# Layer 1 in the order of every fourth token, layer 0 entries turned by DMA, and new latencies in the list of a four-layer graph kernel

## The chip, the cores and the metric

One core of one Trainium2 chip. The time is the device time of one execution in microseconds; for the kernel before it is the median of three runs, 1753.9 us (1751.21 to 1754.06).

## The reference

Input x holds 32 graphs of 512 tokens with 128 features; adj is one 512 x 512 matrix of zeros and ones for all of them. Each of four layers computes x = x + layer(relu(layernorm(x)), adj).

```python
# layer 0: attention by edges
x_h = elu(x @ Wi + bi)
a_src, a_tgt = x_h @ We[:H, 0], x_h @ We[H:, 0]
e = sigmoid(a_tgt[:, :, None] + a_src[:, None, :] + be) * (adj + ALPHA * (adj == 0))
recv = elu(concat([einsum('bij,bjh->bih', e, x_h), x_h * e.sum(-1, keepdims=True)]) @ Wn + bn)
out = concat([recv, x_h]) @ Wm + bm
# layer 1: a gated unit, five steps (in_matrix = out_matrix = adj)
m = adj @ h;  av = concat([m, m]);  u3 = h @ u3_w.T + u3_b
z = sigmoid(av @ w3_w.T + w3_b + u3);  r = sigmoid(av @ w4_w.T + w4_b + u3)
hv = tanh(av @ w5_w.T + w5_b + (r * h) @ u5_w.T + u5_b);  h = (1 - z) * h + z * hv
# layer 2: adj @ (x @ weight) + bias
# layer 3: sum over k = 0..3 of adj^k @ x @ V_k, V_k folded from weight_1
```

## The kernel before, in words

All tensors stay in fp32; x of four graphs (a group, G = 4) lies in one "x" buffer of [128, 4, 4, 128], tokens on partitions in four chunks. Inside a layer most tiles are feature-major: features on the 128 partitions, the 512 tokens in the free dimension ("f" buffers, 36 of them; "b" buffers are the eight PSUM banks, "m" and "d" are scratch in DRAM).

**A list, not loops, sets the order.** `Plan.op` (L53) records every operation with its engine, an estimate of its duration, a due time and what it reads and writes. `Plan.order` (L98) then plays the list through: an engine that is free takes the ready operation with the earliest due time for which buffers are free. A result counts as known `RESULT[eng]` (L45) after the operation's end. An operation of DVE that is marked `two` (two inputs in SBUF) and any of POOL exclude each other in it. The instructions are then issued in that order on every engine. The due times come from `begin(b)` (L560), from PACE, FIRST_PACE and LAST_PACE (L217) and from offsets in each layer. [...]

**Prefix and arms.** Up to `BRANCH` (30 us of the list) the order is common (L578). In this prefix adj is transposed into A_r (fp32r), a mask is made, and four DVE operations (L424) count elements that fp32r would not hold exactly; all engines read the count `inexact` and branch (L812). Of the two arms the exact one runs with these inputs: each value for an adjacency product is split in fp32r parts `hi` (ACT, L672) and `lo` (DVE, L675), and two single-pass matmuls add up to the product.

**Layer 0** (`layer0`, L455): layernorm (L377 to L404: statistics on DVE, the power on POOL, scaling on ACT), then h is turned to feature-major by four TensorE transposes into a PSUM bank (`transposed`, L324) and an ACT copy (`copied`, L350), and multiplied with Wi (`product`, L355). elu (L440) takes three activations and two DVE operations. For the edges, four times a tanh (L507) and a DVE operation with the mask (L510); POOL adds the four results (L516, three additions). TensorE forms the messages (L525), and one product with ones (L530, graphs 0 to 3; issued at L357) or two fp32r passes (L539, later graphs) form the sum over neighbours; own (L542), Wn (L357), elu, and Wm (L552) follow.

**Layer 1** (`layer1`, L694): h is feature-major. In each of the five steps the adjacency product (L686, eight passes) and u3T (L357) come first, each copied out of PSUM by ACT (L352); then gate r (w4T, L704, L362, L711), gate z (w3T), w5T and u5T into one bank, a tanh, and three DVE operations (L721, L723, L725). `turned` (L333) brings h back to tokens on partitions: one DVE transpose of 32 x 32 blocks (L337), a DMA to scratch (L340) and a DMA back (L342). L337 reads its source with a step of four elements, which is why the blocks' rows are every fourth token.

**Layers 2 and 3** (L737, L751): one adjacency product and a narrow product; and a Horner scheme over k with L760 and L769.

Graphs enter layer 1 at `begin(b)` plus 2.0 PACE, graphs 0 to 3 and the last five at 1.2 PACE (L802).

Of the kernel before, what the change touches and what calls it, by code (L numbers as in the profile page):

```python
# [11 lines left out]
F32R = mybir.dt.float32r  # L12
I32 = mybir.dt.int32
AF = mybir.ActivationFunctionType
ALU = mybir.AluOpType

P = 128
# [21 lines left out]
class Plan:  # L39
# [2 lines left out]

    RESULT = {"PE": 0.5, "ACT": 0.5, "DVE": 0.5, "POOL": 0.6, "SP": 2.5}  # L45

    def __init__(self, slots, ahead, last):
        self.ahead, self.last, self.ops, self.vals = ahead, last, [], {}
# [40 lines left out]
    def back_to(self, state):  # L89
# [5 lines left out]
            )  # L95
        self.free = {k: [*f] for k, f in free.items()}

    def order(self, end=None):  # L98

        left = [o for o in self.ops if not o.begun]  # L100
# [7 lines left out]
        for i, o in enumerate(left):  # L108
            index[o] = i
            o.waits = sum(not b.begun for b in o.before)  # L110
            o.ready = max([0.0, *(b.known for b in o.before if b.begun)])
# [19 lines left out]
        while events:  # L131
            now = heapq.heappop(events)
            if end is not None and now >= end:
                break
            for e in self.until:
                while coming[e] and coming[e][0][0] <= now:
                    _, i, o = heapq.heappop(coming[e])
                    heapq.heappush(ready[e], (o.due, i, o))
                if self.until[e] > now:
                    continue  # L140
                passed, o = [], None
                while ready[e] and o is None:
                    x = heapq.heappop(ready[e])
                    if begins(x[2], now):
                        o = x[2]
                    else:
                        passed.append(x)
                for x in passed:
                    heapq.heappush(ready[e], x)
                if o is None:  # L150
                    continue
                order.append(o)
                o.begun = True
                while oldest + 1 < len(by_due) and by_due[oldest].begun:
                    oldest += 1
                o.start, self.until[e] = now, now + o.us
                if o.two or e == "POOL":
                    self.shared = self.until[e]
                for v in o.takes:
                    v.slot = self.free[v.kind].pop(0)[1]  # L160
                o.known = self.until[e] + o.result
                heapq.heappush(events, self.until[e])
                heapq.heappush(events, o.known)
                for v in o.vals:
                    v.left -= 1
                    if not v.left and v.kind:
                        self.free[v.kind].append((o.known, v.slot))
                        self.free[v.kind].sort()
                for a in o.after:
                    if a in index:  # L170
                        a.waits -= 1
                        a.ready = max(a.ready, o.known)
                        if not a.waits:
                            heapq.heappush(coming[a.eng], (a.ready, index[a], a))
        assert end is not None or len(order) == len(left), "the plan does not end: too few buffers"
# [5 lines left out]
def tile_four_graph_layers(  # L181
# [27 lines left out]
    nc = tc.nc  # L209
# [4 lines left out]
    K = l3_w.shape[2]  # L214
    assert D == P and G * D == 512 and N == 512 and K == 7

    PACE, FIRST_PACE, LAST_PACE = 56.0, 14.0, 30.0  # L217
    BRANCH = 30.0

    T_MM, T_TR, T_NARROW, T_PASS = 0.86, 0.44, 0.224, 0.23  # L220
    T_VEC, T_COPY, T_ACT = 0.61, 0.5, 0.6

    slots = {"x": 6, "f": 36, "q": 4, "s": 8, "d": 4, "m": 8, "b": 8}
    plan = Plan(slots, ahead=60.0, last=(B - 2) * PACE)
    op = plan.op

# [106 lines left out]
    def turned(src, due):  # L333


        blocks, moved, t = Val("f"), Val("m"), Val("f")
        op("DVE", 1.03, due, lambda: nc.vector.transpose(  # L337
            at(blocks).rearrange("p (q c f) -> p q c f", c=NC, f=32),
            at(src).rearrange("p (c i q) -> p q c i", c=NC, q=4)), [src], [blocks])
        op("SP", 1.0, due, lambda: nc.sync.dma_start(at(moved), at(blocks)),  # L340
           [blocks], [moved], result=4.0)
        op("SP", 1.0, due, lambda: nc.sync.dma_start(  # L342
            at(t).rearrange("p (b e) -> p b e", e=P),
            at(moved).rearrange("(b i) (q e) -> (i q) b e", i=32, e=P)), [moved], [t], result=6.0)
        return t

    def by_chunk(t):
# [4 lines left out]
        op("ACT", us, due, lambda: nc.scalar.copy(at(t), at(src)), [src], [t])  # L352
        return t

    def product(w, src, due, dst=None, start=True, stop=True):  # L355
        dst = dst or Val("b")
        op("PE", T_MM, due, lambda: nc.tensor.matmul(  # L357
            at(dst), at(w), at(src), start=start, stop=stop), [src, w], [dst])
        return dst

    def tanh(dst, src, due, bias, scale=0.5, us=T_ACT):
# [45 lines left out]


    A_r, mask = const("A_r", [P, NC, N], F32R), const("mask", [P, NC, N])
    inexact = const("inexact", [1, 1], I32)  # L410
    n_odd = const("n_odd", [P, NC])
    for jc in range(NC):
        pt, z, odd = Val("b"), Val("f"), Val("f")
        def turn(jc=jc, pt=pt):
            for ic in range(NC):
                nc.tensor.transpose(at(pt)[:, ts(ic, P)], at(A_nat[ic])[:, ts(jc, P)], at(ident))
        op("PE", T_TR, jc, turn, [*A_nat, ident], [pt])
        op("ACT", T_COPY, jc, lambda jc=jc, pt=pt: nc.scalar.copy(at(A_r)[:, jc, :], at(pt)),
           [pt], [A_r])
        op("ACT", T_COPY, jc, lambda z=z, pt=pt: nc.scalar.mul(at(z), at(pt), 1 / ALPHA), [pt], [z])  # L420
        op("DVE", T_VEC, jc, lambda jc=jc, z=z, pt=pt: nc.vector.scalar_tensor_tensor(
            at(mask)[:, jc, :], at(pt), 0.0, at(z), op0=ALU.is_equal, op1=ALU.add),
            [pt, z], [mask])
        op("DVE", 0.7, jc, lambda jc=jc, pt=pt, odd=odd: nc.vector.scalar_tensor_tensor(  # L424
            at(odd), at(A_r)[:, jc, :].bitcast(F32), 1.0, at(pt),
            op0=ALU.mult, op1=ALU.not_equal, accum_out=at(n_odd)[:, jc : jc + 1]),
            [A_r, pt], [odd, n_odd])
    p_odd = Val("b")
    def count():
        for jc in range(NC):  # L430
# [4 lines left out]
    op("PE", 0.3, 8, count, [n_odd, ones], [p_odd])  # L435
    op("DVE", 0.2, 8, lambda: nc.vector.tensor_copy(at(inexact), at(p_odd)[:1, :1]),
       [p_odd], [inexact])


# [14 lines left out]

    def layer0(b, h, due):  # L455
        KEEP = 12
        hT = copied(transposed(h, due), due)
        d = due + 6
        xhT = elu(product(Wi_sb, hT, d), bi_sb, bi_half, d, KEEP)

        d = due + 14
        msg, ends = Val("f"), Val("s")
# [42 lines left out]
        for jc in range(NC):  # L505
# [8 lines left out]
        sums = [Val("f"), Val("f")]  # L514
        def add(dst, a, c):
            op("POOL", 1.4, d, lambda: nc.gpsimd.tensor_tensor(  # L516
                at(dst), at(a), at(c), op=ALU.add), [a, c], [dst])
        add(sums[0], es[0], es[1])
        add(sums[1], es[2], es[3])
        add(sums[0], sums[0], sums[1])  # L520

        d = due + 30
        pn = Val("b")
# [3 lines left out]
                [msg, es[jc]], [pn])  # L527

        if b < G:
            ps = product(ones, sums[0], d)  # L530
        else:
            high, low, ps = Val("q"), Val("q"), Val("b")
            op("ACT", T_COPY, d, lambda: nc.scalar.copy(at(high), at(sums[0])), [sums[0]], [high])
            op("DVE", T_VEC, d, lambda: nc.vector.tensor_tensor(
# [54 lines left out]
    def list_rest(exact, pool):  # L589
# [75 lines left out]
        def parts(src, due, two=False, view=None):  # L665
# [3 lines left out]
                return view(at(src)) if view else at(src)  # L669
            def part(v):  # L670
                return at(v).rearrange("p (c b f) -> p c b f", c=NC, f=32) if view else at(v)
            op("ACT", T_COPY, due, lambda: nc.scalar.copy(part(hi), whole()), [src], [hi])  # L672
            if not exact:
                return [hi]
            op("DVE", T_VEC, due, lambda: nc.vector.tensor_tensor(  # L675
# [1 line left out]
                [src, hi], [lo], two=two)  # L677
            return [lo, hi]

        def times_adj(tok, due):  # L680

            pa = Val("b")
            def emit():
                for jc in range(NC):
                    for n, part in enumerate(tok):
                        nc.tensor.matmul(  # L686
                            at(pa), at(part)[:, ts(jc, P)], at(adjT)[:, jc, :],
                            start=jc == n == 0, stop=jc == NC - 1 and n == PARTS - 1,
                        )
            op("PE", NC * PARTS * T_ADJ, due, emit, [*tok, adjT], [pa])  # L690
            return pa


        def layer1(b, h, due, pace):  # L694
            tok = parts(h, due, two=True)
            h = copied(transposed(h, due), due)
            for t in range(STEPS):
                d = due + t * pace
                u = copied(product(u3T, h, d), d)
                m = copied(times_adj(tok, d), d)  # L700

                def gate(wT, bias, d, m=m, u=u):
                    pg, s = product(wT, m, d), Val("f")
# [148 lines left out]
```

## Time and profile before

| what | value |
|---|---|
| median of three runs | 1753.9 us |
| the profiled execution's own time | 1748.12 us |
| its span | 1746.3 us |
| mean granted TensorE clock | 0.994 |
| L686, adjacency of layers 1 and 2 | 1536 matmul records, 421 ns each |
| L357 with u3T, w3T, w4T, w5T, u5T | 320 records each (160 products), 592 to 599 ns |
| L352, ACT copies out of PSUM | 448, 588 ns |
| L516, POOL additions of layer 0 | 96, 1608 ns |
| L399, scaling of layernorm on ACT | 512, 488 ns |

A record of a matmul starts before the one ahead of it has ended, so its duration is longer than the time that it adds; the starts of neighbours tell the latter. One fp32 matmul of 128 x 512 leaves two records. The page divides the span in 40 slices of 43.7 us, and gives for each engine the busy tenths. Groups are given by line, engine and tiles with count, busy us and mean ns, then the idle time of the engine just before them. The chain that ended last is 76% PE.

### The profile page before, as it was taken

Reading aid. Unit: us, or ns where it says so; the run is one execution under the profiler, and the core shown is the slowest. Engines: PE = TensorE matmul, PEld = TensorE weight load, DVE = VectorE, ACT = ScalarE, POOL = GpSimd, SP = SyncE. Lnnn points to the kernel's source line nnn. Section 1 sums busy time; section 2 is a strip of 40 time slices with the busy share of each in tenths; the row PEclk is TensorE's granted clock in tenths of the full one; section 3 lists DMA queues with packets and bytes.
Section 4 is the critical chain, followed back from the end, with each engine's and each line's share of the span. In section 5 each row is a group of like instructions: output and inputs, shape, how many; then the busy total and the mean of one; then the engine's idle time right before and its main releaser. Section 6 shows DMA issues by size and latency. Waiting matters only on the chain.

```text
span 1746.3 us, 21006 instructions
## 1 busy us (share of the span) xinstructions
PE 1695.5 (97%) x6829; PEld 1098.0 (63%) x6829; DVE 1479.3 (85%) x3213; ACT 1135.2 (65%) x2155; POOL 399.8 (23%) x312
## 2 busy tenths in 40 slices
PE   5899999999999999999999999999999999999998
PEld 3555555566666666665666666666666656656797
DVE  6899999999898887888888898888899879878752
ACT  6767765778666666665765667666768656655451
POOL 4521210332222211222212221122232212001110
PEclk9999999999999999999999999999999999999999
DMA  4022322322222222223221221222322131221201
GB/s 109 7 53 75 85 73 73 81 52 85 52 58 61 79 67 46 74 75 55 67 55 60 79 61 61 67 52 81 67 67 55 50 84 61 73 72 58 76 13 48
DMA packets 164534, 112.07 MB, mean 64 GB/s; under 512 B 23232, under 2 KB 139840, under 8 KB 164416
## 3 DMA queue, kind: packets, MB, share of 16 engines
q1 hardware_dynamic: 164416, 110.65, 23.9%
q8 instruction: 55, 0.90, 0.3%
q14 instruction: 63, 0.52, 0.2%
HBM read 60.23 MB, written 50.39 MB: 63 GB/s over the span
## 4 chain that ended last, share of the span: by engine, by line
PE 76%; DVE 13%; DMA 4%; ACT 3%; issue 2%; SPq 0%; DVEq 0%; ACTq 0%
PE b L357 33%; PE b L686 17%; PE b L769 9%; PE b L760 6%; DMA f<-m 4%; PE b L525 4%; PE b L552 3%; DVE f L510 2%; PE b L329 2%; DVE f L704 2%; PE b L743 2%; PE b L469 1%; DVE f L337 1%; DVE f L723 1%; DVE r L675 1%
## 5 line engine op out<-in xcount | busy, mean ns | idle before, releaser
L686 PE MATMUL b<-A_r,r 128*128 128x512 f32 x1536 | 427.6, 421 | 4.3 <-DVE r L675 4.2
L352 ACT COPY f<-b 128x512 f32<-128x512 f32 x448 | 256.5, 588 | 210.6 <-PE b L686 119.2
L686 PEld LDWEIGHTS b<-A_r,r 128*128 128x128 f32 x1536 | 287.2, 189 | 109.6 <-issue 38.9
L391 POOL TENSOR_TENSOR s<-s,nhalf 128x4 f32<-128x4 f32 x128 | 156.2, 1221 | 735.9 <-DVE s L389 707.8
L769 PE MATMUL b<-r,A_r 128*128 128x512 f32 x768 | 306.3, 499 | 0.0
L704 DVE TENSOR_TENSOR f<-f,b 128x512 f32<-128x512 f32 x320 | 213.6, 679 | 56.5 <-PE b L357 54.0
L399 ACT ACTIVATE f<-x,s 128x128 f32<-128x128 f32 x512 | 209.9, 488 | 22.3 <-DVE s L394 22.2
L769 PEld LDWEIGHTS b<-r,A_r 128*128 128x128 f32 x768 | 140.6, 189 | 102.6 <-issue 91.5
L516 POOL TENSOR_TENSOR f<-f,f 128x512 f32<-128x512 f32 x96 | 154.1, 1608 | 207.4 <-DVE f L510 131.1
L362 ACT ACTIVATE f<-f,b4w 128x512 f32<-128x512 f32 x160 | 115.8, 724 | 127.3 <-DVE f L704 126.6
L337 DVE STREAM_TRANSPOSE f<-f 128x512 f32<-128x512 f32 x160 | 176.5, 1105 | 0.3
L675 DVE TENSOR_TENSOR r<-f,r 128x512 fp32r<-128x512 f32 x192 | 141.3, 739 | 37.1 <-ACT r L672 37.0
L357 PE MATMUL b<-f,u5T 128*128 128x512 f32 x320 | 163.2, 595 | 8.7 <-DVE f L711 8.7
L357 PE MATMUL b<-f,w4T 128*128 128x512 f32 x320 | 165.2, 599 | 4.1 <-ACT f L352 4.0
L357 PE MATMUL b<-f,w3T 128*128 128x512 f32 x320 | 163.8, 594 | 0.0
L357 PE MATMUL b<-f,w5T 128*128 128x512 f32 x320 | 163.2, 595 | 0.0
L357 PE MATMUL b<-f,u3T 128*128 128x512 f32 x320 | 162.7, 592 | 0.0
L721 DVE TENSOR_TENSOR f<-f,f 128x512 f32<-128x512 f32 x160 | 121.5, 761 | 39.3 <-ACT f L362 39.1
L760 PEld LDWEIGHTS b<-V,f 128*128 128x128 f32 x1024 | 131.7, 191 | 31.1 <-issue 25.1
L362 ACT ACTIVATE f<-b,b5w 128x512 f32<-128x512 f32 x160 | 109.7, 688 | 60.4 <-PE b L357 60.2
L362 ACT ACTIVATE f<-f,b3w 128x512 f32<-128x512 f32 x160 | 115.0, 721 | 50.8 <-DVE f L704 50.5
L525 PE MATMUL b<-f,f 128*128 128x512 f32 x256 | 130.9, 596 | 3.2 <-issue 3.0
(95 smaller groups left out, 2489.9 us busy)
## 6 DMA issues: line engine op xcount, KB each, us to landing
m<-f SPq DMA_DIRECT2D x160, 256.0 KB, 2.0
f<-m SPq DMA_DIRECT2D x160, 256.0 KB, 2.8
x<-in_x_dram SPq DMA_DIRECT2D x32, 256.0 KB, 4.5
out_dram<-x SPq DMA_DIRECT2D x32, 256.0 KB, 2.4
f<-d SPq DMA_DIRECT2D x28, 256.0 KB, 4.1
f<-in_adj_dram SPq DMA_DIRECT2D x4, 256.0 KB, 4.6
f<-in_L_gnn_weight_dram SPq DMA_DIRECT2D x2, 224.0 KB, 2.6
d<-s SPq DMA_DIRECT2D x28, 2.0 KB, 9.1
```

Of the source, the lines that this page charges most:

```text
L337: op("DVE", 1.03, due, lambda: nc.vector.transpose(at(blocks).rearrange("p (q c f) -> p q c f", c=NC, f=32), at(src).rearrange("p (c i q) ...
L352: op("ACT", us, due, lambda: nc.scalar.copy(at(t), at(src)), [src], [t])
L357: op("PE", T_MM, due, lambda: nc.tensor.matmul(at(dst), at(w), at(src), start=start, stop=stop), [src, w], [dst])
L362: op("ACT", us, due, lambda: nc.scalar.activation(at(dst), at(src), AF.Tanh, bias=at(bias), scale=scale), [src, bias], [dst])
L391: op("POOL", 1.2, due, lambda: nc.gpsimd.tensor_tensor(stat(SCALE), stat(VAR), at(neg_half), op=ALU.pow), [s, neg_half], [s])
L399: nc.scalar.activation(at(h)[:, ts(c, P)], at(X[b])[:, c, :], AF.Relu, bias=stat(SHIFT)[:, c : c + 1], scale=stat(SCALE)[:, c : c + 1],)
L525: op("PE", T_MM, d, lambda jc=jc: nc.tensor.matmul(at(pn), at(msg)[:, ts(jc, P)], at(es[jc]), start=jc == 0, stop=False), [msg, es[jc]], [pn])
L675: op("DVE", T_VEC, due, lambda: nc.vector.tensor_tensor(part(lo), whole(), part(hi).bitcast(F32), op=ALU.subtract), [src, hi], [lo], two=two)
L686: nc.tensor.matmul(at(pa), at(part)[:, ts(jc, P)], at(adjT)[:, jc, :], start=jc == n == 0, stop=jc == NC - 1 and n == PARTS - 1,)
L704: op("DVE", T_VEC, d, lambda: nc.vector.tensor_tensor(at(s), at(u), at(pg), op=ALU.add), [u, pg], [s])
L760: nc.tensor.matmul(at(pz)[:, ts(i, D)], at(hT[i])[:, ts(ic, P)], at(V[k]), start=i == 0, stop=last and i == G - 1,)
L769: nc.tensor.matmul(at(pz), at(adjT)[:, jc, ts(ic, P)], at(part), start=False, stop=jc == NC - 1 and n == PARTS - 1,)
```

## The change

- **Order of layer 1.** The columns of h and of everything feature-major in layer 1 stand in the order of every fourth token: token 128c + 4i + q at place (c, q, i). A copy of the adjacency in that order, A_fours, is made by four ACT copies in the prefix, and the adjacency product of layer 1 reads it. The ACT copy of h out of PSUM, once per graph, puts h in that order with a strided read. The DVE transpose in `turned` reads runs of 32 values now.
- **Entry of layer 0.** Graphs 4 to 31 no longer use TensorE transposes and an ACT copy: `turned_back` takes a DVE transpose of 32 x 32 blocks with a strided read and two DMAs by way of scratch. Their product with Wi writes its columns back in natural order by an access pattern. The due times of what follows are 6 us later.
- **Sums of graphs 0 to 3.** Four products with ones, one for each of the four edge results, in place of three POOL additions and one product.
- **List.** RESULT falls to 0.25 (PE) and 0.2 (ACT, DVE, POOL), nothing is added between operations of one engine (`known`), DMAs of `turned` count 0.45 us of SP with results 2.6 and 3.6 us later (before 1.0, 4.0 and 6.0); FIRST_PACE is 10 in place of 14; graphs 0 to 3 enter layer 1 at 0.75 PACE; the counting of inexact elements is due at 8; POOL additions of later graphs are due 10 earlier; `hi` copies leave one buffer free; x has 5 buffers in place of 6.

```diff
-    RESULT = {"PE": 0.5, "ACT": 0.5, "DVE": 0.5, "POOL": 0.6, "SP": 2.5}
+    RESULT = {"PE": 0.25, "ACT": 0.2, "DVE": 0.2, "POOL": 0.2, "SP": 2.5}
...
+    def known(self, o, to):
+
+        return o.known - o.result if to.eng == o.eng != "SP" else o.known
...
-                        a.ready = max(a.ready, o.known)
+                        a.ready = max(a.ready, self.known(o, a))
...
-    PACE, FIRST_PACE, LAST_PACE = 56.0, 14.0, 30.0
+    PACE, FIRST_PACE, LAST_PACE = 56.0, 10.0, 30.0
...
-    T_VEC, T_COPY, T_ACT = 0.61, 0.5, 0.6
-
-    slots = {"x": 6, "f": 36, "q": 4, "s": 8, "d": 4, "m": 8, "b": 8}
+    T_VEC, T_COPY, T_ACT, T_DMA = 0.61, 0.5, 0.6, 0.45
+
+    slots = {"x": 5, "f": 36, "q": 4, "s": 8, "d": 4, "m": 8, "b": 8}
...
     def turned(src, due):
...
+        blocks, moved, t = Val("f"), Val("m"), Val("f")
+        op("DVE", 0.63, due, lambda: nc.vector.transpose(
+            at(blocks).rearrange("p (q c f) -> p q c f", c=NC, f=32),
+            at(src).rearrange("p (c q i) -> p q c i", c=NC, q=4)), [src], [blocks])
+        op("SP", T_DMA, due, lambda: nc.sync.dma_start(at(moved), at(blocks)),
+           [blocks], [moved], result=2.6)
+        op("SP", T_DMA, due, lambda: nc.sync.dma_start(
+            at(t).rearrange("p (b e) -> p b e", e=P),
+            at(moved).rearrange("(b i) (q e) -> (i q) b e", i=32, e=P)), [moved], [t], result=3.6)
+        return t
+
+    def turned_back(src, due):
+
         blocks, moved, t = Val("f"), Val("m"), Val("f")
         op("DVE", 1.03, due, lambda: nc.vector.transpose(
-            at(blocks).rearrange("p (q c f) -> p q c f", c=NC, f=32),
-            at(src).rearrange("p (c i q) -> p q c i", c=NC, q=4)), [src], [blocks])
...
+            at(blocks).rearrange("p (b c i) -> p b c i", c=NC, i=32),
+            at(src).rearrange("p (c f b) -> p b c f", c=NC, b=4)), [src], [blocks])
+        op("SP", T_DMA, due, lambda: nc.sync.dma_start(at(moved), at(blocks)),
+           [blocks], [moved], result=2.6)
+        op("SP", T_DMA, due, lambda: nc.sync.dma_start(
+            at(t).rearrange("p (q e) -> p q e", e=P),
+            at(moved).rearrange("(q f) (b e) -> (f b) q e", f=32, e=P)), [moved], [t], result=3.6)
         return t
...
-    def product(w, src, due, dst=None, start=True, stop=True):
+    def product(w, src, due, dst=None, start=True, stop=True, blocks=False):
+
         dst = dst or Val("b")
...
+        def emit():
+            to, of = at(dst), at(src)
+            if blocks:
+                to = to.rearrange("p (c q i) -> p q c i", c=NC, i=32)
+                of = of.rearrange("p (q c i) -> p q c i", c=NC, i=32)
+            nc.tensor.matmul(to, at(w), of, start=start, stop=stop)
+        op("PE", T_MM, due, emit, [src, w], [dst])
...
+    A_fours = const("A_fours", [P, NC, N], F32R)
...
-        op("DVE", 0.7, jc, lambda jc=jc, pt=pt, odd=odd: nc.vector.scalar_tensor_tensor(
+        op("DVE", 0.7, 8, lambda jc=jc, pt=pt, odd=odd: nc.vector.scalar_tensor_tensor(
...
+    for jc in range(NC):
+        op("ACT", 0.52, 30, lambda jc=jc: nc.scalar.copy(
+            at(A_fours)[:, jc, :].rearrange("p (c q i) -> p c q i", c=NC, q=4),
+            at(A_r)[:, jc, :].rearrange("p (c i q) -> p c q i", c=NC, q=4)), [A_r], [A_fours])
...
-        hT = copied(transposed(h, due), due)
+        if b < G:
+            hT = copied(transposed(h, due), due)
+        else:
+            hT = turned_back(h, due)
+            due += 6
         d = due + 6
-        xhT = elu(product(Wi_sb, hT, d), bi_sb, bi_half, d, KEEP)
+        xhT = elu(product(Wi_sb, hT, d, blocks=b >= G), bi_sb, bi_half, d, KEEP)
...
         if b < G:
-            ps = product(ones, sums[0], d)
+            ps = Val("b")
+            for jc in range(NC):
+                product(ones, es[jc], d, ps, start=jc == 0, stop=jc == NC - 1)
         else:
+            sums = [Val("f"), Val("f")]
+            def add(dst, a, c):
+                op("POOL", 1.4, d - 10, lambda: nc.gpsimd.tensor_tensor(
+                    at(dst), at(a), at(c), op=ALU.add), [a, c], [dst])
...
-            op("ACT", T_COPY, due, lambda: nc.scalar.copy(part(hi), whole()), [src], [hi])
+            op("ACT", T_COPY, due, lambda: nc.scalar.copy(part(hi), whole()), [src], [hi],
+               keep=1)
...
-        def times_adj(tok, due):
+        def times_adj(tok, due, fours=False):
...
+            columns, view = adjT, lambda t: t
+            if fours and exact:
+                columns = A_fours
...
         def layer1(b, h, due, pace):
             tok = parts(h, due, two=True)
-            h = copied(transposed(h, due), due)
+            pt, h = transposed(h, due), Val("f")
+            op("ACT", T_COPY, due, lambda h=h, pt=pt: nc.scalar.copy(
+                at(h).rearrange("p (c q i) -> p c q i", c=NC, q=4), at(pt).rearrange("p (c i q) -> p c q i", c=NC, q=4)), [pt], [h])
...
-                m = copied(times_adj(tok, d), d)
+                m = copied(times_adj(tok, d, fours=True), d)
...
-                t = begin(b) + (2.0 if G <= b < B - G - 1 else 1.2) * PACE
+                t = begin(b) + (0.75 if b < G else 2.0 if b < B - G - 1 else 1.2) * PACE
```

More of the change, by code (lines that the diff above doesn't have):

```diff
@@ L110, in order @@
             o.waits = sum(not b.begun for b in o.before)
-            o.ready = max([0.0, *(b.known for b in o.before if b.begun)])
+            o.ready = max([0.0, *(self.known(b, o) for b in o.before if b.begun)])
             if not o.waits:
@@ L336, in turned @@
         blocks, moved, t = Val("f"), Val("m"), Val("f")
-        op("DVE", 1.03, due, lambda: nc.vector.transpose(
-            at(blocks).rearrange("p (q c f) -> p q c f", c=NC, f=32),
-            at(src).rearrange("p (c i q) -> p q c i", c=NC, q=4)), [src], [blocks])
[L340 to L344, printed above, removed]
+        op("DVE", 0.63, due, lambda: nc.vector.transpose(
[9 more added lines that the diff above has]
+        blocks, moved, t = Val("f"), Val("m"), Val("f")
+        op("DVE", 1.03, due, lambda: nc.vector.transpose(
+            at(blocks).rearrange("p (b c i) -> p b c i", c=NC, i=32),
[5 more added lines that the diff above has]
+            at(moved).rearrange("(q f) (b e) -> (f b) q e", f=32, e=P)), [moved], [t], result=3.6)
         return t
@@ L353, in copied @@
         return t
-    def product(w, src, due, dst=None, start=True, stop=True):
+    def product(w, src, due, dst=None, start=True, stop=True, blocks=False):
         dst = dst or Val("b")
-        op("PE", T_MM, due, lambda: nc.tensor.matmul(
-            at(dst), at(w), at(src), start=start, stop=stop), [src, w], [dst])
+        def emit():
[5 more added lines that the diff above has]
+        op("PE", T_MM, due, emit, [src, w], [dst])
         return dst
@@ L434, in count @@
             )
-    op("PE", 0.3, 8, count, [n_odd, ones], [p_odd])
-    op("DVE", 0.2, 8, lambda: nc.vector.tensor_copy(at(inexact), at(p_odd)[:1, :1]),
+    op("PE", 0.3, 9, count, [n_odd, ones], [p_odd])
+    op("DVE", 0.2, 9, lambda: nc.vector.tensor_copy(at(inexact), at(p_odd)[:1, :1]),
        [p_odd], [inexact])
@@ L513, in layer0 @@
             es.append(e)
[L514 to L520, printed above, removed]
         d = due + 30
@@ L529, in layer0 @@
         if b < G:
-            ps = product(ones, sums[0], d)
-        else:
+            ps = Val("b")
+            for jc in range(NC):
+                product(ones, es[jc], d, ps, start=jc == 0, stop=jc == NC - 1)
+        else:
+            sums = [Val("f"), Val("f")]
+            def add(dst, a, c):
+                op("POOL", 1.4, d - 10, lambda: nc.gpsimd.tensor_tensor(
+                    at(dst), at(a), at(c), op=ALU.add), [a, c], [dst])
+            add(sums[0], es[0], es[1])
+            add(sums[1], es[2], es[3])
+            add(sums[0], sums[0], sums[1])
             high, low, ps = Val("q"), Val("q"), Val("b")
@@ L678, in parts @@
             return [lo, hi]
-        def times_adj(tok, due):
+        def times_adj(tok, due, fours=False):
             pa = Val("b")
+            columns, view = adjT, lambda t: t
+            if fours and exact:
+                columns = A_fours
+            elif fours:
+                view = lambda t: t.rearrange("p (c i q) -> p c q i", c=NC, q=4)
             def emit():
@@ L686, in emit @@
                         nc.tensor.matmul(
-                            at(pa), at(part)[:, ts(jc, P)], at(adjT)[:, jc, :],
+                            at(pa), at(part)[:, ts(jc, P)], view(at(columns)[:, jc, :]),
                             start=jc == n == 0, stop=jc == NC - 1 and n == PARTS - 1,
                         )
-            op("PE", NC * PARTS * T_ADJ, due, emit, [*tok, adjT], [pa])
+            op("PE", NC * PARTS * T_ADJ, due, emit, [*tok, columns], [pa])
             return pa
```

## The prediction

> **What bounds the kernel now.** I read the page's busy shares and slices first, then the time line of TensorE, the windows by stage, the waits of TensorE, and last the groups.
>
> The page (busy us with share, then 40 slices of 43.7 us in tenths):
>
> ```profile
> PE 1695.5 (97%) x6829; PEld 1098.0 (63%) x6829; DVE 1479.3 (85%) x3213; ACT 1135.2 (65%) x2155; POOL 399.8 (23%) x312
> ...
> PE   5899999999999999999999999999999999999998
> ...
> DVE  6899999999898887888888898888899879878752
> ```
>
> TensorE is full from the third slice on. Ends of matmuls are modelled, so I check by starts in the time line (start, us, engine, line):
>
> ```profile
> 503.77 0.60 PE L329 MATMUL b<-ident,f 128*128 128x128 f32 x4
> 504.20 1.02 PE L357 MATMUL b<-f,u3T 128*128 128x512 f32 x2
> 505.07 1.02 PE L357 MATMUL b<-f,Wi_sb 128*128 128x512 f32 x2
> 505.92 1.02 PE L357 MATMUL b<-f,u5T 128*128 128x512 f32 x2
> ```
>
> Start to start, one product (two records) takes 0.86 us and four transposes 0.43. In the same way a pass of L686, L769 or L539 takes 0.23 and a record of L760, L552, L469 or L743 0.112. Counts times these: 1736 records of L357 and 256 of L525 at 0.43, 2360 passes at 0.23, 2048 narrow ones at 0.112, 384 transposes at 0.109, small rest 5: 1675 us. TensorE first starts at 6.3 us and its last start lies 5.0 before the end of the span. So 1746.3 - 6.3 - 5.0 - 1675 = 60 us are stalls and slow clock: all that a new order of work can win. The same count up to 89 us gives 23 us; the other 37 lie in 89 to 1741. The windows (each engine's busy us, granted clock, DMA):
>
> ```profile
> 6.30:30.00 23.70, 13.05 (x55) 9.47 (x56) 12.27 (x50) 17.11 (x36) 8.75 (x10) 0.86 0.34 89
> 30.00:50.00 20.00, 15.87 (x75) 9.62 (x75) 19.61 (x44) 14.30 (x31) 12.59 (x13) 1.00 0.27 74
> 50.00:70.00 20.00, 18.03 (x73) 9.75 (x71) 18.62 (x47) 14.87 (x30) 13.40 (x11) 1.00 0.01 2
> ...
> 89.00:1600.00 1511.00, 1489.02 (x5769) 941.41 (x5768) 1330.74 (x2813) 1011.67 (x1905) 335.51 (x242) 1.00 0.25 66
> ...
> 926.00:942.00 16.00, 13.92 (x47) 8.24 (x45) 14.93 (x27) 6.12 (x12) 5.41 (x4) 0.89 0.10 33
> ```
>
> The third column is DVE: from 30 to 70 us it is busy 38.2 of 40 us, so the start of the run is DVE's, not TensorE's, with POOL busy 26 us beside it. The last row shows one of four places (near 314, 804, 929, 1428 us) where TensorE stood still for about 2 us and the clock then was 0.5 for 3.4 us.
>
> The waits of TensorE (total us, times, longest):
>
> ```profile
> PE b L357 <- DVE f L711: 8.7, 8, 2.1
> ...
> PE b L552 <- DVE f L451: 4.4, 3, 3.0
> PE b L686 <- DVE r L675: 4.2, 4, 2.1
> PE b L357 <- ACT f L352: 4.0, 2, 2.2
> ```
>
> Few, and mostly for DVE: what comes late is a vector result.
>
> [...] L337 reads every fourth fp32, 16 bytes apart; its record is 1105 ns against 732 to 761 of L721 to L725 on the same 128x512 f32[...]. [...] L510 (two SBUF inputs) has a mean of 900 ns although two of them start 0.60 apart at 24.8 us, before POOL's additions begin[...]. [...]
>
> **The change part by part.** The rows:
>
> ```profile
> L337 DVE STREAM_TRANSPOSE f<-f 128x512 f32<-128x512 f32 x160 | 176.5, 1105 | 0.3
> ...
> L510 DVE SCALAR_TENSOR_TENSOR f<-f,mask 128x512 f32<-128x512 f32 x128 | 107.8, 900 | 7.4 <-ACT f L507 3.8 <-ACT f L447 3.5
> ...
> m<-f SPq DMA_DIRECT2D x160, 256.0 KB, 2.0
> f<-m SPq DMA_DIRECT2D x160, 256.0 KB, 2.8
> ```
>
> 1. *Layer 0 of graphs 4 to 31 enters by DMA.* 28 x 4 transposes leave TensorE: 28 x 0.43 = -12.0 us, on the bound engine in its full stretch, so it counts whole. ACT loses 28 copies (28 x 0.48 = 13 us), DVE gains 28 strided transposes (28 x 1.1 = 31 us), SP 56 DMAs on top of 376. The entry takes 1.1 + 0.3 + 2.0 + 0.4 + 2.8 = 6.6 us, instead of some 1.3; the list places the consumers 6 us later, and TensorE has other graphs' work. If that cover is gone, a graph costs up to 5 us. DMA engines go from 24% to about 27%. On SP, loads and stores stand behind two more waits per graph; L342's waits for the first landing cost SP 272 us in 124 waits, so 28 more cost it some 60, in a queue that otherwise mostly waits. The matmul with Wi writes PSUM in runs of 32: no row for it; between 0 and one more 0.43 per record, 28 x 0.86 = 24 us; I take 0[...].
> 2. *Sums of graphs 0 to 3 on TensorE.* 16 products with ones instead of 4: 12 x 0.86 = +10.3 us, but before 89 us, where TensorE has 23 us of stalls. 12 POOL additions go (12 x 1.6 = 19 us)[...]: 16 of L510 at 0.60 instead of about 0.9, up to 5 us of DVE there.
> 3. *Layer 1 in fours.* 160 transposes read in runs of 32 values. Not in the trace: between 0 and 1105 - 679 = 0.43 us saved each; I take 0.37, 59 us of DVE. With the 31 of part 1 DVE loses 28 us, 2%. Off the path; it shortens a chain between two steps of a graph, which has 20 us of TensorE work as median cover. Price of this by itself: nothing directly. A_fours costs four ACT copies, between 4 x 0.5 and twice that for the stride; they stand ahead of the tanh of graph 0, so up to 2 to 4 us in the start. The layer-1 copy of h reads PSUM with a stride, 32 times, at most 0.5 more: 16 us of an ACT busy 65%.
> 4. *The list.* In the order of the built kernels graph 0's first DVE step of elu stood behind four countings and the statistics of four graphs; now two countings and two graphs' statistics lie behind it: 2 x 0.60 + 2 x 1.15 = 3.5 us earlier; less the A_fours copies, plus the two scalings of x that no longer precede its tanh (3.2 us). FIRST_PACE 10 and the due times of layer 1 at 0.75 PACE draw graphs 0 to 3 together: the first adjacency product of layer 1 comes after 38 us of TensorE work instead of 43. The smaller T_DMA and results of SP, the POOL additions of later graphs due 10 us earlier and keep=1 on the parts move list positions only; what they can cost is the thinner cover of the slower rival. The branch (3 us of idle on DVE and PE near 27 us) stays.
> 5. *x buffers 6 to 5.* The load of group 5 now needs the store of group 0; about 200 us of TensorE work lie between. Nothing; if not, 4.5 us per load.
>
> Start: 2 and 4 give 3 us of head start for graph 0 and 5 us of freed DVE and POOL waits. I take 8 of its 23 us; from +4 (the A_fours copies with no gain) to -14. The 10.3 us of part 2 are counted as work. Steady stretch: DVE 2% lighter, but covers thinner (below); I take -2 of 37, from -15 to +25.
>
> Sum: -12.0 + 10.3 - 8 - 2 = -12. The profiled execution took 1748.1 (span 1746.3), so it would be 1736; the runs' median is 1753.9, 5.8 above it, and I carry the difference over: 1742.
>
> **Rivals.**
> - *Slower: covers too thin.* The list now counts 0.2 us for a result where it had 0.5. I summed, in both orders, the TensorE work between a producing and a consuming group less the durations of the vector steps between: of some 1620 groups, 53 had under 1 us to spare before and 84 have it now, under 2 us 151 and 267; the Wn product behind the ones sum falls from 1.7 to 0.8 us in the median, w4T and w3T behind the adjacency from 2.7 to 1.9. A DVE operation held by POOL comes up to 1 us late, as L510's mean shows, and a stall of 2 us costs 1.7 more by the clock. It decides when the steady stalls pass 37 + 10 = 47 us. At 37 + 22: -1.7 - 8 + 22 = +12, 1766. For it: the waits named above are for DVE already. Against: the trace's own gap from end to start is 0.04 to 0.08, and records exceed spacing by 0.08 to 0.17, so 0.2 and 0.25 still cover it.
> - *The start doesn't shorten* because ACT (17.1 of 23.7 busy before 30 us) and the branch hold it: -1.7 and a few us of either sign, 1752: no change.
> - *Both shrink:* start -12, steady stalls -14 with fewer slow-clock spells: 1726. For it: DVE lighter where waits are for DVE.
>
> **How the numbers follow.** About 0.2% (3.5 us) is what a measurement of this kernel can tell. Forecast (1733 to 1749) 0.46; both shrink 0.20; no change 0.11; slower 0.23. Faster 0.66, same 0.11, slower 0.23. Range for 8 in 10: 1723 to 1764, from the better rival's time, less 3 for its own spread, to within the slower rival's, of which some half lies beyond, so that about 0.2 is left out in all; the likeliest case's own range is 1733 to 1749.
>
> **What would show it.** Right: 112 transposes fewer in L333; the transposes of turned near 0.7 us; TensorE stalls before 89 us near 15 us with DVE under 95% there; no more than four half-clock spells after 89 us. Wrong: waits of TensorE for the DVE steps of elu and of the r gate summing to over 30 us; transposes still at 1.1 us; waits for the DMAs of turned_back on the TensorE row.

## The result and the profile after

The changed kernel takes 1902.6 us in the median against 1753.0 of the kernel before (now over four runs): a ratio of 1.0853, with a 95% interval from 1.0831 to 1.0875. The forecast was 1742. The profiled execution has a span of 1902.5 us.

The page of the kernel after, busy times and slices:

```profile
PE 1745.7 (92%) x6741; PEld 1105.0 (58%) x6741; DVE 1464.2 (77%) x3241; ACT 1128.2 (59%) x2131; POOL 373.4 (20%) x300
...
PE   6988898998988999889989899988999898999998
...
DVE  5778788998867788677878678867788877788752
```

TensorE's row of nines is broken all along the run, not in one place, and DVE, which was the late engine before, has more idle time than it had. The same windows as before:

```profile
6.30:30.00 23.70, 14.22 (x50) 9.61 (x51) 13.93 (x52) 18.69 (x35) 6.46 (x9) 0.71 0.33 89
30.00:50.00 20.00, 17.61 (x64) 9.12 (x63) 11.58 (x39) 15.05 (x34) 5.87 (x9) 1.00 0.16 40
50.00:70.00 20.00, 20.00 (x78) 11.66 (x77) 14.48 (x32) 15.40 (x32) 8.07 (x11) 1.00 0.24 76
89.00:1600.00 1511.00, 1378.88 (x5137) 852.24 (x5136) 1202.42 (x2613) 910.42 (x1722) 311.36 (x231) 0.96 0.27 68
```

The start did get lighter: DVE is busy 26 of 40 us from 30 to 70 us where it was busy 38. From 89 to 1600 us TensorE does 5137 matmul records where it did 5769, at a mean clock of 0.96. Counted as in the prediction, by starts: the loss up to 89 us is 24.2 us in the kernel before (the prediction has 23) and 19.7 in the kernel after; the loss from 89 us on is 37.3 before and 198.7 after. All of the result lies in that last number. Half-clock time is 23.9 us in 6 spells before and 140.8 us in 25 spells after. Past 89 us, TensorE's gaps of over 0.1 us grow from 22.6 to 132.8 us in the traces, and its busy time under the half clock from 13.5 to 95.3 us, of which about half is lost (the two records of a product start 0.85 us apart there in the median and 0.43 at full clock): together 151 of the 161 us.

What TensorE waits for in the kernel after; then ACT's wait for a DMA, in the kernel after and in the kernel before, where the same line is L672. `m<-f` is the first DMA of a turn, to scratch; `f<-m` is the second, back:

```profile
PE b L381 <- ACT f L370: 67.9, 16, 6.1
PE b L381 <- DVE f L755: 40.1, 21, 5.9
```
```profile
ACT r L708 <- DMA f<-m: 153.0, 29, 9.6
```
```profile
ACT r L672 <- DMA f<-m: 23.0, 8, 3.7
```

The wait for L370 (the ACT copy of the adjacency product m) is new in this size: 4.0 us in 2 waits before. In these places ACT is not held by work of its own; it stands at L708, the `hi` copy of a turned h, until the second DMA of `turned` has landed: 153.0 us in 29 waits, against 23.0 in 8 before. One such place in the time line of the kernel after (start, us, engine, line):

```profile
1298.77 0.38 SPq L522 DMA_DIRECT2D d<-s  x1
...
1300.61 0.36 SPq L347 DMA_DIRECT2D f<-m  x1
...
1311.18 0.62 ACT L708 CAST r<-f 128x512 fp32r<-128x512 f32 x1 [6.08 <-DMA f<-m]
1311.70 1.06 ACT L370 COPY f<-b 128x512 f32<-128x512 f32 x2
...
1312.34 2.08 PE L381 MATMUL b<-f,w4T 128*128 128x512 f32 x2 [5.44 <-ACT f L370]
```

The gather `d<-s` of layer 0 (a column of scores to a row, 512 pieces of 4 bytes) is issued, and 1.8 us later the second DMA of a turn; that one lands 10.5 us after its issue. ACT waits 6.1 us in front of L708, the copy of m stands behind it on ACT, TensorE waits 5.4 us for the copy, and then its two records take 2.08 us where they take 1.02 at full clock. This is no single case: 25 of the 28 gathers, which come about every 55 us, are followed within 20 us by a TensorE gap of over 1 us, 109 us in all. Before the change it was 5 of 28, and 9 us.

The slow landings were there before the change. For the DMAs of the turns (and of `turned_back`) the views by tile give, for the kernel before and the kernel after:

```profile
DMA to landing us min/median/max: 2.0/2.7/12.2
```
```profile
DMA to landing us min/median/max: 2.0/2.8/12.0
```

Of 245 whose landing the trace of before tells, 28 took over 5 us, all issued within 10.5 us after a gather; after the change 47 of 376, 45 of them after a gather. What changed is what the list has ready for it, its cover: the time that it leaves between a result and its use. Before, a turn's DMAs counted 5 and 7 us from the start of the issue to a known result; after, 3.05 and 4.05, which is near the medians, 2.0 and 2.9, and far from the late ones.

### The profile page after: what moved, and what is told of

The parts are those of the page before. It is cut to its first block, busy times and chain, and to the rows that moved or that the text cites. A ratio compares the mean times of both kernels' runs of the same rounds, so it can differ in the third digit from the quotient of the medians.

```text
span 1902.5 us, 20910 instructions
## 1 busy us (share of the span) xinstructions
PE 1745.7 (92%) x6741; PEld 1105.0 (58%) x6741; DVE 1464.2 (77%) x3241; ACT 1128.2 (59%) x2131; POOL 373.4 (20%) x300
## 4 chain that ended last, share of the span: by engine, by line
PE 38%; DVE 12%; DMA 9%; ACT 4%; issue 1%; DVEq 0%; SPq 0%; ACTq 0%
PE b L381 16%; DMA f<-m 7%; PE b L728 7%; PE b L813 6%; PE b L804 4%; PE b L552 2%; DMA m<-f 2%; ACT f L386 1%; DVE f L767 1%; DVE f L765 1%; DVE f L748 1%; PE b L588 1%; ACT f L423 1%; DVE f L544 1%; DVE r L712 1%
## 5 line engine op out<-in xcount | busy, mean ns | idle before, releaser
L728 PE MATMUL b<-A_fours,r 128*128 128x512 f32 x1280 | 379.7, 439 | 1.5 <-DVE r L712 1.5
L728 PEld LDWEIGHTS b<-A_fours,r 128*128 128x128 f32 x1280 | 241.1, 190 | 110.0 <-issue 60.3
L370 ACT COPY f<-b 128x512 f32<-128x512 f32 x388 | 222.4, 584 | 130.0 <-PE b L728 76.2
L381 PE MATMUL b<-f,w4T 128*128 128x512 f32 x320 | 178.4, 642 | 66.8 <-ACT f L370 66.8
L813 PE MATMUL b<-r,A_r 128*128 128x512 f32 x768 | 215.6, 419 | 0.0
L381 PE MATMUL b<-f,u5T 128*128 128x512 f32 x320 | 172.7, 624 | 40.1 <-DVE f L755 40.1
L708 ACT CAST r<-f 128x512 fp32r<-128x512 f32 x192 | 117.6, 620 | 153.4 <-DMA f<-m 153.0
L381 PE MATMUL b<-f,w3T 128*128 128x512 f32 x320 | 175.4, 634 | 0.0
L563 POOL TENSOR_TENSOR f<-f,f 128x512 f32<-128x512 f32 x84 | 126.9, 1511 | 219.0 <-DVE f L544 158.8
L804 PE MATMUL b<-V,f 128*128 128x128 f32 x1024 | 134.9, 278 | 0.0
```

The costliest lines, as they stand in the source:

```text
L381: nc.tensor.matmul(to, at(w), of, start=start, stop=stop)
L563: op("POOL", 1.4, d - 10, lambda: nc.gpsimd.tensor_tensor(at(dst), at(a), at(c), op=ALU.add), [a, c], [dst])
L728: nc.tensor.matmul(at(pa), at(part)[:, ts(jc, P)], view(at(columns)[:, jc, :]), start=jc == n == 0, stop=jc == NC - 1 and n == PARTS - 1,)
L804: nc.tensor.matmul(at(pz)[:, ts(i, D)], at(hT[i])[:, ts(ic, P)], at(V[k]), start=i == 0, stop=last and i == G - 1,)
L813: nc.tensor.matmul(at(pz), at(adjT)[:, jc, ts(ic, P)], at(part), start=False, stop=jc == NC - 1 and n == PARTS - 1,)
```

## Experiments

Each kernel is compared with the kernel before on the same chip (1746.2 to 1746.6 us there), so ratios are the numbers to compare. Theory A: late landings behind the gather, and a list without cover for them. Theory B, the rival: results of 0.2 and 0.25 us leave too thin a cover between engines whatever the DMAs do. Theory C: the entry by DMA is the load. In the later runs theory A' is A with two layers of cover, the turns' DMA numbers and the results between engines.

**The turns listed as before**

```diff
-    T_VEC, T_COPY, T_ACT, T_DMA = 0.61, 0.5, 0.6, 0.45
+    T_VEC, T_COPY, T_ACT, T_DMA = 0.61, 0.5, 0.6, 1.0
...
-           [blocks], [moved], result=2.6)
+           [blocks], [moved], result=4.0)
...
-            at(moved).rearrange("(b i) (q e) -> (i q) b e", i=32, e=P)), [moved], [t], result=3.6)
+            at(moved).rearrange("(b i) (q e) -> (i q) b e", i=32, e=P)), [moved], [t], result=6.0)
...
```
The two DMAs of `turned_back` get the same numbers.

> The kernel after, with the two DMAs of each turn (layer 1 and layer 0 entry) listed as before the change: 1.0 us of SP each, results 4.0 and 6.0 us later; nothing else is changed. Theory A (the turns' DMAs that stand behind the 4-byte gather d<-s land 8 to 10 us late, and the list with 2.6 and 3.6 leaves no cover for it): 1735 to 1775 us, waits of the hi copies L708 for f<-m under 50 us. Theory B (results of 0.2 and 0.25 us leave too thin a cover between engines): still over 1870. Theory C (the layer 0 entry by DMA itself is the load): still over 1850.

1779.2 us, ratio 1.0191 [1.0170, 1.0211].

```profile
ACT r L708 <- DMA f<-m: 49.2, 23, 5.7
```

Three quarters of the loss go, though 56 landings are over 5 us here, so that theories B and C, which had over 1870 and over 1850, miss. The time stays a little above what A gave. What counts is the cover, not how many DMAs are late.

**The older results between engines**

```diff
-    RESULT = {"PE": 0.25, "ACT": 0.2, "DVE": 0.2, "POOL": 0.2, "SP": 2.5}
+    RESULT = {"PE": 0.5, "ACT": 0.5, "DVE": 0.5, "POOL": 0.6, "SP": 2.5}
...
-        return o.known - o.result if to.eng == o.eng != "SP" else o.known
+        return o.known
```


> The kernel after, with RESULT of the kernel before (0.5, 0.5, 0.5, 0.6) and without the rule that a result costs nothing on its own engine; the turns' DMAs stay at 0.45 with 2.6 and 3.6. Theory A: still over 1860, waits of L708 for f<-m over 100 us. Theory B: 1740 to 1780. Theory C: over 1850.

1791.6 us, 1.0261 [1.0241, 1.0281]: A's number for this run was wrong, and B's and C's too.

```profile
ACT r L708 <- DMA f<-m: 109.7, 31, 8.3
```

ACT still waits over 100 us for f<-m, but TensorE stands still for 75 us in gaps over 0.1 us where it stood 151. So ACT's waits reach TensorE less; that the wide results put more work between ACT's late copy and the product that needs it is the likely reason, but was not counted. The two sets of latencies act like two layers of one cover: either one takes most of the loss away.

**The gather from another queue**

```diff
-                nc.sync.dma_start(
+                nc.scalar.dma_start(
...
-            op("SP", 0.6, due + 10, gather, [ends], [row], result=11.0)
+            op("ACT", 0.1, due + 10, gather, [ends], [row], result=11.0)
```


> The kernel after, with the gather d<-s issued from the ACT queue instead of SP's, so that the turns' DMAs no longer stand behind it in their queue; the list's numbers stay. Theory A, if it is the queue's order that holds them: 1730 to 1770, and no f<-m or m<-f over 6 us. If the 512 small pieces hold the DMA engines themselves, the late landings stay and so does the time, over 1860. Theory B and C: over 1850.

1868.4 us, 1.0690 [1.0672, 1.0708]; 45 landings over 5 us. Two lines of this kernel, the gather by tile and the wait of ACT:

```profile
L522 ACTq DMA_DIRECT2D d<-s x28: 366/366/388, 84.0 to 1545.0; - x28
```
```profile
ACT r L708 <- DMA f<-m: 130.3, 27, 7.4
```

The gather is on ACT's queue now and nearly as many turns are late as before (47): the order within a queue is not what holds them.

**The turns' new numbers alone, in the kernel before**

```diff
-        op("SP", 1.0, due, lambda: nc.sync.dma_start(at(moved), at(blocks)),
-           [blocks], [moved], result=4.0)
-        op("SP", 1.0, due, lambda: nc.sync.dma_start(
+        op("SP", 0.45, due, lambda: nc.sync.dma_start(at(moved), at(blocks)),
+           [blocks], [moved], result=2.6)
+        op("SP", 0.45, due, lambda: nc.sync.dma_start(
...
-            at(moved).rearrange("(b i) (q e) -> (i q) b e", i=32, e=P)), [moved], [t], result=6.0)
+            at(moved).rearrange("(b i) (q e) -> (i q) b e", i=32, e=P)), [moved], [t], result=3.6)
```


> The kernel before, with only the listing of the turns' two DMAs changed to 0.45 us of SP and results 2.6 and 3.6. Theory A: the loss appears here too, 1810 to 1900, with PE waits of 3 to 6 us after gathers. Theory B and C: within 1% of the kernel before.

1752.8 us, 1.0041 [1.0031, 1.0051]: far less than A said, and what B and C gave. With the wide results left in, little is lost; but in this list only 12 of 283 known landings are over 5 us, so the one layer was not tried as hard here as in the kernel after.

**Both new sets in the kernel before**

```diff
-    RESULT = {"PE": 0.5, "ACT": 0.5, "DVE": 0.5, "POOL": 0.6, "SP": 2.5}
+    RESULT = {"PE": 0.25, "ACT": 0.2, "DVE": 0.2, "POOL": 0.2, "SP": 2.5}
...
+    def known(self, o, to):
+
+        return o.known - o.result if to.eng == o.eng != "SP" else o.known
...
-                        a.ready = max(a.ready, o.known)
+                        a.ready = max(a.ready, self.known(o, a))
...
```
With it goes the diff of the run above.

> The kernel before with both sets of new latencies (RESULT 0.25 and 0.2 with the exception on an engine's own results, the turns' DMAs at 0.45 with 2.6 and 3.6), nothing else. Theory A': the loss of the change appears without its other parts, 1830 to 1900, half-clock time over 80 us. If it takes the other parts for the loss: under 1790.

1856.5 us, 1.0622 [1.0600, 1.0645]. Nearly three quarters of the loss (0.062 of 0.085) come from the list's latencies with no other part of the change present. ACT's wait for f<-m in this kernel:

```profile
ACT r L676 <- DMA f<-m: 88.9, 25, 7.3
```

Half-clock time was 73.5 us, a little under the 80 expected.

**Both older sets in the kernel after**

> The kernel after with both sets of latencies of the kernel before: RESULT 0.5, 0.5, 0.5, 0.6, no exception on an engine's own results, and the turns' DMAs at 1.0 us of SP with 4.0 and 6.0; the order in fours, the entry by DMA, the ones products and the due times stay. Theory A' (the late landings behind the gather are there in both kernels, and the list's latencies are the cover against them, in two layers that add): 1725 to 1755, half-clock time under 30 us. If the entry by DMA or the other parts cost something of their own: over 1765.

The edit is the first two of this section together. 1728.7 us, 0.9893 [0.9876, 0.9909], faster than the kernel before and with 24.6 us of half-clock time, as theory A' had it. From its TensorE waits:

```profile
PE b L381 <- DVE f L755: 6.9, 7, 2.0
...
PE b L381 <- ACT f L370: 0.5, 1, 0.5
```

All that is left of the change, that is the order in fours, the entry by DMA, the ones products, the due times and the buffers, is together a gain of about 1%: 17.5 us.

**The entry by TensorE**

```diff
-        if b < G:
-            hT = copied(transposed(h, due), due)
-        else:
-            hT = turned_back(h, due)
-            due += 6
+        hT = copied(transposed(h, due), due)
         d = due + 6
-        xhT = elu(product(Wi_sb, hT, d, blocks=b >= G), bi_sb, bi_half, d, KEEP)
+        xhT = elu(product(Wi_sb, hT, d), bi_sb, bi_half, d, KEEP)
```


> The kernel after with all graphs entering layer 0 by TensorE transposes and an ACT copy (turned_back is not used, due times as for graphs 0 to 3), 56 DMAs fewer. Theory A': still over 1840, since the layer 1 turns stand behind the gather as before. Theory C (the entry's DMAs are the load): under 1790.

1847.3 us, 1.0582 [1.0564, 1.0600]. Theory C falls as the main cause; ACT waits for turns without the entry's DMAs too:

```profile
ACT r L704 <- DMA f<-m: 102.1, 29, 8.8
```

The entry by DMA as a whole (56 DMAs and due times 6 us later, in place of transposes and copies) makes the loss larger, by 0.027 of the ratio, within a list that has no cover.

**The gather made short**

```diff
...
-                nc.sync.dma_start(
-                    at(row).rearrange("o (c p) -> p (o c)", c=NC), at(ends)[:, NC : 2 * NC]
-                )
+                for k in range(NC):
+                    nc.sync.dma_start(
+                        at(row).rearrange("o (c k i) -> k (o c) i", c=NC, k=NC)[k],
+                        at(lines)[32 * k + NC : 32 * k + 2 * NC, :32],
+                    )
...
-            op("SP", 0.6, due + 10, gather, [ends], [row], result=11.0)
+            op("DVE", 0.14, due + 10, lambda: nc.vector.transpose(
+                at(lines)[:, :32], at(ends)[:, :32]), [ends], [lines])
+            op("SP", 1.8, due + 10, gather, [lines], [row], result=11.0)
...
```


> The kernel after with its list as it is, but the gather d<-s made short: a DVE transpose of 32 columns first, then four DMAs of four pieces of 128 bytes in place of one DMA of 512 pieces of 4 bytes. Theory A': what is late is taken away, so 1730 to 1770 with no f<-m over 6 us, although the list has no cover. If thin covers between engines cost by themselves (theory B): over 1800 with f<-m all near 3 us.

1750.1 us, 1.0020 [1.0013, 1.0027]: the loss is gone with the latencies as they are, as theory A' had it, and B's over 1800 misses. The trace of this kernel does not tell landings, so I read who waits; ACT, then SP's own wait for the first DMA of a turn (longest 3.6 us, where it was 10.9):

```profile
ACT r L716 <- DMA f<-m: 0.3, 1, 0.3
```
```profile
SPq L351 <- DMA m<-f: 196.1, 134, 3.6
```

So in this list the late landings cost some 0.083 of the ratio, about 145 us. The edit also changes the list a little (the transpose, and 1.8 us of SP for the gather in place of 0.6, which moves turns behind it), but the DMA packets show that the lateness itself is gone, and not only covered: in the kernel after, 272 of the 130304 packets of 512 bytes took over 1 us; in this kernel, with as many packets, none did. The late landings come from the gather's 512 pieces.

**What thin cover costs without late landings.** Three kernels with the short gather, by the edits above: the turns' DMAs listed long; the older results; both.

> The short gather with the new RESULT and only the turns' DMAs at the older 1.0 with 4.0 and 6.0. Theory A': without late landings the DMA numbers matter little, 1735 to 1750 (1750.1 with the new ones). If what remains of the loss is turns that are late by a little: under 1735.

> The short gather with the older RESULT and no exception on an engine's own results, the turns' DMAs at 0.45 with 2.6 and 3.6. Theory B, as a remainder (thin covers between engines cost some us by themselves, with no late DMA): 1715 to 1735, below 1750.1 by 15 us or more. If they cost nothing: 1743 to 1757.

> The kernel after with the short gather (a DVE transpose, four DMAs of four pieces of 128 bytes) and both sets of the older latencies. Theory A': no late landing and full cover: 1710 to 1728, below the 1728.7 of the same list with the long gather. If the landings were fully covered there already: within 0.2% of it.

The last column has the same list with the long gather, from the runs above:

| short gather with | us | ratio | ratio with the long gather |
|---|---|---|---|
| both new (the run above) | 1750.1 | 1.0020 [1.0013, 1.0027] | 1.0853 |
| turns long, results new | 1746.3 | 1.0001 [0.9993, 1.0010] | 1.0191 |
| turns short, results old | 1717.4 | 0.9835 [0.9816, 0.9854] | 1.0261 |
| both old | 1724.3 | 0.9872 [0.9854, 0.9890] | 0.9893 |

The gather's late landings cost 0.083 with no cover, 0.019 and 0.043 with one layer, and 0.002 with both, where the intervals overlap. The loss belongs to neither alone: it takes late landings and a list without cover. Of the expectations, A' is right for the first of the three and B, as a remainder, for the second; for the third the two cases can't be told apart.

With no late landings the turns' numbers matter little, and not in one direction (the short ones lose 4 us with the new results and gain 7 with the older ones), while the new results still cost 33 us: theory B is right as the smaller part. The waits of TensorE for the r gate (L763 here), in the kernel with both new and in the one with the older results:

```profile
PE b L385 <- DVE f L763: 11.6, 11, 1.8
```
```profile
PE b L385 <- DVE f L763: 4.4, 6, 1.0
```

A last kernel splits the 33 us: the short gather with older values and the new rule on an engine's own results.

```diff
-    RESULT = {"PE": 0.25, "ACT": 0.2, "DVE": 0.2, "POOL": 0.2, "SP": 2.5}
+    RESULT = {"PE": 0.5, "ACT": 0.5, "DVE": 0.5, "POOL": 0.6, "SP": 2.5}
```

> The short gather with the older RESULT values (0.5, 0.5, 0.5, 0.6) but the new rule that a result costs nothing between operations of one engine; the turns' DMAs at 0.45 with 2.6 and 3.6. It splits the 33 us between 1750.1 (both new) and 1717.4 (both old). If the values between engines are the cover: 1712 to 1725. If it is the rule on an engine's own results: 1740 to 1755.

1727.9 us, 0.9893 [0.9877, 0.9910]: between the two, above the 1712 to 1725 of the first case. By this split the values account for 22 us of the 33 and the rule for 10. But each new number in the list changes the whole order, and the turns' numbers alone moved the time by 4 us one way and 7 the other, so the 10 us are not shown to be the rule's.

The kernel with the short gather, the older results and the turns at 2.6 and 3.6 is faster than both kernels of the study.

## Why the prediction was wrong

**Part 1, entry by DMA.** The counts held: 272 records of transposes in place of 384, and Wi's product with its new output pattern takes 604 ns per record against 594, with starts 0.43 us apart in both kernels, so the 0 that the prediction took, its author's estimate, held. SP's waits for the 28 new first landings were put at some 60 us and took 123.5. That the entry would gain its 12 us did not hold in the list as it was made: it cost 0.027 of the ratio there, some 47 us. The prediction had named this case, up to 5 us for each of the 28 graphs if the cover is gone, but not counted it. In the list with both layers of cover the whole rest of the change gained 17.5 us, so it can't have cost much there; no run takes the entry alone out of that list.

**Part 2, sums, and the start.** The right sign, about half the size: the loss before 89 us fell by 4.5 us, not 8, and the first matmul came 0.7 us later, since the transposes of h now stand ahead of those of adj.

**Part 3, fours.** Right. The groups of the kernel after:

```profile
L342 DVE STREAM_TRANSPOSE f<-f 128x512 f32<-128x512 f32 x160 | 112.2, 705 | 2.1
...
L355 DVE STREAM_TRANSPOSE f<-f 128x512 f32<-128x512 f32 x28 | 30.9, 1105 | 4.9 <-ACT f L423 4.7
```
```profile
L455 ACT CAST A_fours<-A_r 128x512 fp32r<-128x512 f32 x4 | 4.1, 1093 | 0.0
```

Runs of 32 save 0.40 us each (0.37 taken), the strided one costs 1105 as before, and the four A_fours copies cost 4.1 us, the upper bound of the estimate. The strided copy of h out of PSUM takes 594 ns, about as long as a plain one (584).

**Part 4, the list: here it failed.** The prediction put the smaller DMA numbers down as moving "list positions only", left what they can cost to the slower rival, which then reckoned with results between engines alone, and put the steady stretch at -2 with bounds of -15 and +25. It measured +161. I had costed DMAs by their medians, 2.0 and 2.8 us, and did not ask for their spread, although the view by tile above has a longest landing of 12.2 us, and the gather's own row stands a few rows below the medians in the list from which these came:

```profile
d<-s SPq DMA_DIRECT2D x28, 2.0 KB, 9.1
```

The waits of TensorE before the change didn't name a DMA because the list's 4.0 and 6.0, which looked like a loose estimate, were together with the wide results the cover for just these landings. ACT's waits named it already, 23.0 us in 8. The rest of the forecast was near: with both older sets of latencies the change gains 17.5 us, where the prediction's sum was -12.

**The slower rival** had the right place, covers too thin, and the right further cost, the clock (140.8 us at half clock against 23.9). Its size of +22 is near what thin results cost without late DMAs (33 us), and far from the 145 us of the DMAs; that it is near is in part chance, for it named POOL's hold on DVE as what comes late (in the kernel before, L510 took 671 to 1783 ns, 1137 in the mean, in the 61 cases with a POOL operation running beside it, and 637 to 694 in the other 67), and no run singles that out, while the largest wait is for an ACT copy behind a DMA. The prediction's own sign of being wrong, over 30 us of waits for the r gate and elu, was met, 40.1 for L755 alone, but not for its reason: 33 of these 40.1 us lie within 20 us after a gather.

**x buffers.** No load of x waited for the store of an earlier group in the SP view; right.

Open stays how the pieces delay others within the DMA engines. In the packets of one gather at 1298.8 us, its 4-byte pieces ran within 2 us of its issue, at 7 ns each, while the 512-byte packets of the DMAs behind it (a turn's and a store's) came thinly until about 10 us after it, the slowest taking 2.0 us against a median of 27 ns. What held them no run shows.

## What to carry to other kernels

Where a list fixes the order on every engine, a planned latency is cover, and it has to come from the late landings (here up to 12.0 us), not from the median (2.0 and 2.9): ask the trace for the longest one, what was issued just before it, and which engine has its next work behind the wait (here ACT, with the copy of m behind a wait of 6.1 us). Take the late one away at its source before the cover is cut. And a list whose numbers are true on average may still want some tenths of a microsecond more between engines: here 0.5 beat 0.2 by 22 us, and by 33 with the older rule on an engine's own results.

## What the runs showed of the hardware

- A DMA of 2 KB in 512 pieces of 4 bytes took 8.6 to 11.9 us to land in the kernel after, and 45 of the 48 turns' DMAs of 256 KB issued within 10.5 us behind it took over 5 and up to 12.0 us, where the medians of all are 2.0 and 2.9. Issued from ACT's queue, it still left 45 landings over 5 us. With the same 2 KB in 16 pieces of 128 bytes no 512-byte packet took over 1 us, where 272 had.
- Past 89 us in the kernel after, each of the 23 half-clock spells before the run's end came with or just after a stall of TensorE of 1.9 to 6.1 us, while four stalls of 2.6 to 3.4 us brought none, so the length of a stall alone does not decide. In the kernel before, stalls of 1.8 to 2.2 us were enough. Of the 23 spells, 10 lasted 3.4 us and 13 lasted 6.8.
- DVE's 32 x 32 transpose of 128x512 fp32 took 705 ns with runs of 32 values and 1105 with a step of 16 bytes; ACT's copy of that size took 1093 with that step from SBUF and 594 from PSUM.
